# Decay buffers taken strictly in turn, decays first in ScalarE's order, and four steps of the plan moved by one scan

## The chip, the core and the metric

The kernel runs on one core of one Trainium2 chip. The metric is the device time of one execution in microseconds. Before the change, the median of three runs is 29332.89 us (29323.41 to 29336.83).

The engines are named as in the profile: PE (TensorE, with PEld for its weight loads), DVE (VectorE), ACT (ScalarE), POOL (GpSimd) and SP (SyncE, which here issues all DMAs). Each engine works through its own queue in order, so an instruction that waits holds up all that stand behind it on that engine.

## What is computed

The input is eight images of 64 channels by 128 by 128. Two layers follow each other. Cut to what matters here:

```
# layer 0: a learned high-pass filter, nine weights a pixel
h    = leaky(conv3x3(x, w1));  w_lp = softmax(conv1x1(h, w2) over the 9 taps)
x    = x + sum over taps of shifted(x) * (delta - w_lp)
# layer 1: norms, then two bidirectional state space blocks over the 16384 pixels of an image
for each block, for each direction:
    xc = silu(causal_conv1d(x));  dt = softplus(...);  B, C = projections of xc
    state[d, n] = exp(dt[d] * A[d, n]) * state[d, n] + dt[d] * B[n] * xc[d]     # along the pixels
    y[d] = sum over n of state[d, n] * C[n] + D[d] * xc[d];  y *= silu(z)
# then "mix": two 3x3 convolutions, a product and a norm; then an FFN:
g = depthwise3x3(conv1x1(x, 340 channels));  out = x + conv1x1(gelu(g1) * g2)
```

With 128 channels d and 16 states n there are 2048 recurrences a direction, each 16384 pixels long.

## The kernel before, in words

**Chunks and scans.** The recurrences run on DVE. A chunk is 1024 pixels of one direction of one block of one image; there are 512 chunks, each with 16 scans of 128 recurrences by 1024 pixels, so 8192 scans in all. Scan `u` of a chunk needs:

- `decay` (L1118): one ACT instruction that writes exp(dt * A) into a PSUM tile `w` of two banks;
- `drive` (L1110): POOL's product `bu` of dt * xc and B, one instruction for two scans, four buffers;
- `scan` (L1136 forwards, L1138 backwards): one DVE instruction. Its result goes into the tile `hs` if POOL is to multiply by C, else back into `w` in place;
- `product` by C: on POOL (L1157, about a third of the scans: u even, not 4 or 12, and 8 only beside other work), else on DVE (L1160), from `w` into `hs`;
- `keep` (L1150): a small ACT copy of the last column into `state`. For a POOL product it stands right after the scan and POOL waits for it; for a DVE product it stands after the product;
- `collect` (L1176): PE sums over n into a PSUM tile `y`, which `y_out` reads in halves (L1193 on ACT in a first direction, L1191 on DVE in a second one).

**One time axis.** All work is placed by hand: `at(time, phase, step)`, where a unit of time is one scan and scan `u` of a chunk that begins at `b` stands at `b + u`. Steps are issued in order of time, within a time by phase (FEED, SCAN, MID, PROD, DECAY, REST), and within a phase in the order of the calls. That gives each engine's queue. `decay(u)` stands at `b + u - 2`, two scans ahead, in phase DECAY, behind what an earlier chunk put into the same time and phase.

**The two buffers of `w`.** The tiles come from a pool of PSUM with two buffers under one tag (`ps_w`, tag "w"), and the framework gives each new tile the buffer that its own scheduling model expects to be free first. In the program as built, 7773 decays get the other buffer than the decay before them, and 419 get the same one: 377 of these at u = 3 or u = 11, all of them after a scan whose product is on POOL. A decay in the same buffer has to wait until the scan just before its own has read it.

**Beside the scans** three streams of other work run, each at its own time of the image (an image is 1024 scans): the *front* of the next image (layer 0 and the first norms, one piece each 24 scans, times 569 to 985 of an image), the *mix* of the image itself (a piece each 13 scans, from time 992 for 208 scans, so into the next image's first 176) and the *FFN* of the image before (a piece each 24 scans, times 180 to 569). Their convolutions are PE work. Of the front, the softmax over taps matters here: `less_max` on DVE and `exps` (L539) on ACT at time b + 23, `sums` (L543, L544: a reduction and a reciprocal on DVE) at b + 24, `softmax` (L547 on POOL) at b + 24, then three `piece`s (L551 on ACT) with `less_piece` (L555 on POOL) between them, and a PE transposition. Of the FFN: four parts of `conv` (L819, L825 on PE) at a + 14 to a + 17 fill two PSUM banks, `times` (L881, two DVE products with the gelu) at a + 19 reads them, `project` (PE) at a + 19, `add` (L903 on ACT) and `store` at a + 21.

**DMAs.** SP issues everything, in order. The tiles of C (`load_states("cp", ...)`, L1088, four DMAs of 256 KB for half of the states) have one buffer a half; the half that a chunk needs from its scan 4 on is loaded at time b, after the last product of the chunk before has read the old one.

At the start nine pieces of the front and at the end the last FFN stand alone, without scans beside them; they use the `ps_w` buffers too.

Of the kernel before, what the change touches and what calls it, by code (L numbers as in the profile page):

```python
# [8 lines left out]
F32 = mybir.dt.float32  # L9
# [4 lines left out]
PSUM = bass.MemoryType.PSUM  # L14

P = 128
# [14 lines left out]
T = 1024  # L31
# [2 lines left out]
G = 4  # L34
U = G * G
PW = W + 2
FEED, SCAN, MID, PROD, DECAY, REST = range(6)

IMAGE = 4 * NT * U
FRONT_STEP, MIX_STEP, FFN_STEP = 24, 13, 24  # L40
# [2 lines left out]
SILU, SOFTPLUS, GELU = 11, 18, 11  # L43
# [12 lines left out]
def kernel(ctx: ExitStack, tc: tile.TileContext, a: dict, out: bass.AP):  # L56
# [134 lines left out]
    with tc.tile_pool(name="wspill", bufs=1) as fp, tc.tile_pool(name="wprep", bufs=2) as pp, \  # L191
            tc.tile_pool(name="wps", bufs=4, space=PSUM) as pps:
        with tc.manual_schedule():
# [126 lines left out]
            for l in range(DEPTH):  # L320
# [17 lines left out]
                for d in range(2):  # L338
# [3 lines left out]
                    for j in range(KC):  # L342
                        t = turned(taps[:, j, :], ident, P, DI)
                        at = j if d == 0 else KC - 1 - j
# [51 lines left out]
    def at(time, phase, fn, *args):  # L396
        steps.setdefault((time, phase), []).append((fn, args))
# [1 line left out]
    inp = ctx.enter_context(tc.tile_pool(name="in", bufs=2))  # L399
    wk = ctx.enter_context(tc.tile_pool(name="wk", bufs=2))  # L400
    sd = ctx.enter_context(tc.tile_pool(name="between", bufs=3, space=bass.MemoryType.DRAM))
    pw = ctx.enter_context(tc.tile_pool(name="ps_w", bufs=2, space=PSUM))
    py = ctx.enter_context(tc.tile_pool(name="ps_y", bufs=1, space=PSUM))
    pm = ctx.enter_context(tc.tile_pool(name="ps_mm", bufs=1, space=PSUM))
    pb = ctx.enter_context(tc.tile_pool(name="ps_bg", bufs=1, space=PSUM))
    pa = ctx.enter_context(tc.tile_pool(name="ps_acc", bufs=1, space=PSUM))

    def mm_tile(name):
        return pm.tile([P, N], F32, tag="mm", name=name)
# [87 lines left out]
    class Front:  # L497
# [68 lines left out]
        def weight(self, k):  # L566
            if not self.alone:
                self.wb = bg_tile("wb")
            else:
                if k % 2 == 0:  # L570
                    self.wbs = pw.tile([P, T], F32, tag="w", name="wb")
                self.wb = self.wbs[:, N * (k % 2) : N * (k % 2) + N]
            self.wbk[k] = self.wb
            nc.tensor.matmul(self.wb, sel_k[:, k].rearrange("k h c -> k (h c)"), self.wt, start=True, stop=True)
# [73 lines left out]
        def plan(self, a):  # L648
            n1, n2, n3 = self.n1, self.n2, self.n3
            b = a - FRONT_STEP  # L650
            self.alone = a + FRONT_STEP < -2
            at(b - 5, REST, self.load_xa)
            for i in range(3):
                at(b + 1 + i, REST, self.hidden, i)
            at(b + 6, DECAY, self.hidden_out)
            at(b + 21, REST, self.logits)
            at(b + 23, DECAY, self.less_max)
            at(b + 23, DECAY, self.exps)
            at(b + 24, DECAY, self.sums)
            at(b + 24, REST, self.softmax)  # L660
            for i in range(3):
                at(b + 26 + 2 * i, DECAY, self.piece, i)
                if i < 2:
                    at(b + 27 + 2 * i, REST, self.less_piece, i)
            at(b + 31, REST, self.turn)
            at(b + 32, DECAY, self.turned)
            at(a + 6, REST, self.load_xb)
            for k in range(9):

                t = a + k + (k >= 3)  # L670
                at(t + 11, REST, self.weight, k)
                at(t + 12, MID, self.weighted, k)
                at(t + 13, REST, self.gather, k)
            at(a + 23, DECAY, self.filtered)
            at(a + 23, REST, self.store_x1)
            at(a + 23, REST, self.centered, acc_tile, "x1")
            at(a + 24, DECAY, self.centered_out)
            at(a + 25, REST, lambda: n1.means(bg_tile, self.sq))
            at(a + 26, DECAY, n1.means_out)
            at(a + 26, REST, n1.root)  # L680
            at(a + 28, REST, n1.spread, bg_tile)
            at(a + 29, MID, self.scaled, n1)
            at(a + 29, DECAY, self.first_norm)
            at(a + 30, REST, self.pointwise)
            at(a + 31, DECAY, self.pointwise_out)
            at(a + 31, REST, self.store_rows, dw_img[self.p], "dwt")
            at(a + 31, REST, self.centered, acc_tile, "xn")
            at(a + 32, DECAY, self.centered_out)
            at(a + 33, REST, lambda: n2.means(acc_tile, self.sq))
            at(a + 34, DECAY, n2.means_out)  # L690
            at(a + 34, REST, n2.root)
            at(a + 36, REST, n2.spread, acc_tile)
            at(a + 37, MID, self.scaled, n2)
            at(a + 37, DECAY, self.second_norm)
            at(a + 37, REST, self.store_h)
            at(a + 38, REST, lambda: n3.means(bg_tile, self.sq))
            at(a + 39, DECAY, n3.means_out)
            at(a + 39, REST, n3.root)
            at(a + 47, REST, n3.spread, bg_tile)
            at(a + 49, MID, self.third_norm)  # L700
            at(a + 49, REST, self.store_hn)
# [81 lines left out]
    class Ffn:  # L783
# [15 lines left out]
        def conv(self, g, part):  # L799

            wpair, wlast, _, _, _, _ = ffn_weights(Bg.weights)
            if part == 0 and self.alone:
                w = pw.tile([P, T], F32, tag="w", name="fp")
                self.p = [w[:, 0:N], w[:, N:T]]
            elif part == 0:
                self.p = [acc_tile("fp"), bg_tile("fp")]
            if g == 2:
                self.rest = self.p
            outs = []
            for h in range(2):  # L810
                if g < 2:
                    outs += [(self.p[h], h, slice(0, P))]
                else:
                    outs += [(self.p[0][C * h : C * h + C, :], h, slice(C, P))]
            for h in range(2 * (g == 2)):
                outs += [(self.p[1][C * h : C * h + C, :], h, slice(0, C))]
            for i in ((0,), (1,), (2,), ())[part]:
                for o, h, m in outs:
                    nc.tensor.matmul(  # L819
                        o, wpair[:, i, g, m], self.win[h][:, i : i + ROWS, 0:W], start=(i == 0), stop=False  # L820
                    )
            for i in ((), (), (0,), (1, 2))[part]:
                for o, h, m in outs:
                    rows, lo = slice(C * h, C * h + C), 2 - h
                    nc.tensor.matmul(  # L825
                        o, wlast[rows, i, g, m], self.win[h][rows, i : i + ROWS, lo : W + lo],
                        start=False, stop=(i == 2),
                    )
# [83 lines left out]
        def plan(self, a):  # L912
            early = 12 if self.alone else 0
            at(a - 4 - early, REST, self.load, 0)
            at(a - 3 - early, REST, self.load, 1)

            if self.alone:
                at(a - 6, REST, self.before_taps)
                at(a - 5, DECAY, self.before_taps_out)
                at(a - 5, REST, self.taps, 0)  # L920
                at(a - 2, REST, self.taps, 1)
                groups = ((0, 0, self.first_out, 2), (3, 1, self.times, 6))
                gelus, out = 3, 9
            else:
                groups = ((0, 0, self.first_out, 5), (6, 2, None, 0), (14, 1, self.times, 19))
                gelus, out = GELU, 19
            for t, g, end, to in groups:
                for i in range(4):
                    at(a + t + (0 if self.alone else i), REST, self.conv, g, i)
                for h in range(2 if end else 0):  # L930
                    at(a + to, MID if end == self.times else DECAY, end, h)
            at(a + gelus, REST, self.gelus)
            at(a + gelus + 2, MID, self.rest_times)
            at(a + out - 5, REST, self.load_x2)
            at(a + out, REST, self.project)
            at(a + out + 2, DECAY, self.add)
            at(a + out + 2, REST, self.store)
# [15 lines left out]
    class Chunk:  # L953
# [159 lines left out]
        def decay(self, u):  # L1113
            k, i = divmod(u, 2)
            j, gp = self.pairs[k]
            g = 2 * gp + i
            w = pw.tile([P, T], F32, tag="w", name="w")
            nc.scalar.activation(  # L1118
                w, self.dtp[gp][:, i, :], AF.Exp, scale=a_neg[:, self.l, self.d, g, j : j + 1]
            )  # L1120
            self.ws[u] = w
# [115 lines left out]
        def plan(self):  # L1237
            b = self.t0 - 2 * U
# [20 lines left out]
            b = self.t0  # L1259
# [11 lines left out]
            at(b - 4, REST, self.load_states, "cp", j0)  # L1271
            at(b - 3, REST, self.load_channels, "dup", 1)
            at(b - 2, REST, self.load_channels, "dtp", 1)
            at(b + 0, REST, self.load_states, "cp", 1 - j0)
            for k in range(U // 2):
                at(b + 2 * k - 5, REST, self.drive, k)
                at(b + 2 * k + 3 + (k % 4 == 0), REST, self.collect, k)
            for u in range(U):
                at(b + u - 2, DECAY, self.decay, u)
                at(b + u, SCAN, self.scan, u)  # L1280
                at(b + u + self.on_pool(u), FEED if self.on_pool(u) else PROD, self.product, u)
            for h in range(2):
# [76 lines left out]
```

## Time and profile before

| what | value |
|---|---|
| median of three runs | 29332.89 us |
| the profiled execution's own time | 29319.34 us |
| span of its profile | 29317.6 us |
| PE busy | 23234.6 us (79%) |
| DVE busy | 27195.5 us (93%) |
| ACT busy | 18546.6 us (63%) |
| POOL busy | 27646.8 us (94%) |
| decays, L1118 on ACT | 8192 of 1118 ns (median) |
| scans, L1136 and L1138 on DVE | 8192 of about 2345 ns |
| products, L1160 on DVE and L1157 on POOL | 5360 of 1221 ns and 2832 of 2358 ns |
| drives, L1110 on POOL | 4096 of 4538 ns |
| DMA engines, mean busy share of the hardware queue | 71.0% |
| first scan and last scan start | 507 us and 28869 us |

The profile is one execution. Its page gives the busy time of each engine, which counts neither semaphores nor the issuing of DMAs, then groups of instructions with the idle time of the engine just before them and what ended that. The view of waits sums this by pairs: "engine line waited for: us in total, times, longest us". A window is a stretch of the span in us. A time line has the start, the duration, the engine and line, and in square brackets the idle time before and its releaser.

### The profile page before, as it was taken

How to read it: one execution, taken by the hardware profiler on the slowest of the kernel's cores; microseconds unless marked ns; L12 is line 12 of the kernel's file. 1: busy time of each engine (PE TensorE's matmuls, PEld its weight loads, DVE VectorE, ACT ScalarE, POOL GpSimd, SP SyncE). 2: the span in 40 equal slices, each digit the busy share in tenths (PEclk: the TensorE clock that was granted, in tenths of full speed). 3: DMA queues.
4: the chain of work that ended last, by engine and by line, in shares of the span. 5: the costliest groups of instructions: out<-in, count | busy, mean ns of one | idle time of the engine just before them, and what ended most of it. 6: DMA issues, size and time to landing. Idle time of an engine off the chain costs nothing. (4 is left out here: it accounts for less than half of the span.)

```text
span 29317.6 us, 309769 instructions
## 1 busy us (share of the span) xinstructions
PE 23234.6 (79%) x97708; PEld 7300.4 (25%) x97708; DVE 27195.5 (93%) x17567; ACT 18546.6 (63%) x28361; POOL 27646.8 (94%) x8732
## 2 busy tenths in 40 slices
PE   6666888878788787887878778787787877878678
PEld 3211222222222222222322223222222222222123
DVE  4999999999999999999999999999999999999997
ACT  3666666666666666666666666666666666666663
POOL 3999999999999999999999999999999999999994
PEclk7777888988899888998889889898888988889789
DMA  4676777767777678776787767777677776777674
GB/s 121 224 241 217 228 250 244 239 218 230 253 240 238 216 234 258 239 237 214 234 258 240 233 217 239 252 241 230 218 240 252 240 228 220 246 249 238 218 250 142
DMA packets 2592261, 6762.65 MB, mean 231 GB/s; under 512 B 431270, under 2 KB 736822, under 8 KB 2589462
## 3 DMA queue, kind: packets, MB, share of 16 engines
q1 hardware_dynamic: 2590614, 6742.83, 71.0%
q8 instruction: 773, 12.66, 0.2%
q14 instruction: 874, 7.16, 0.1%
HBM read 5509.49 MB, written 1265.19 MB: 231 GB/s over the span
## 5 line engine op out<-in xcount | busy, mean ns | idle before, releaser
L1110 POOL TENSOR_TENSOR bu<-dup,bp 128x2048 f32<-128x2048 f32 x4096 | 18558.9, 4538 | 15.9 <-DMA dup<-du_dram 7.2
L1118 ACT ACTIVATE w<-dtp,a_neg 128x1024 f32<-128x1024 f32 x8192 | 9159.0, 1118 | 750.6 <-DVE hs L1136 360.6
L1157 POOL TENSOR_TENSOR hs<-hs,cp 128x1024 f32<-128x1024 f32 x2832 | 6679.1, 2358 | 618.0 <-ACT state L1150 557.5
L1160 DVE TENSOR_TENSOR hs<-w,cp 128x1024 f32<-128x1024 f32 x5360 | 6546.4, 1221 | 254.9 <-DMA cp<-bc_dram 73.2
L1136 DVE TENSOR_TENSOR_SCAN w<-w,state,bu 128x1024 f32<-128x1024 f32 x2677 | 6280.0, 2346 | 313.5 <-ACT w L1118 311.9
L1138 DVE TENSOR_TENSOR_SCAN w<-w,state,bu 128x1024 f32<-128x1024 f32 x2683 | 6289.6, 2344 | 293.8 <-ACT w L1118 292.7
L1176 PE MATMUL y<-hs,sel_y 128*32 128x512 f32 x32768 | 5055.5, 691 | 66.8 <-POOL hs L1157 66.4
L1150 ACT COPY state<-w 128x1 f32<-128x1 f32 x5360 | 837.1, 156 | 5943.6 <-DVE hs L1160 5873.0
L1138 DVE TENSOR_TENSOR_SCAN hs<-w,state,bu 128x1024 f32<-128x1024 f32 x1413 | 3308.1, 2341 | 145.8 <-issue 57.7
L1136 DVE TENSOR_TENSOR_SCAN hs<-w,state,bu 128x1024 f32<-128x1024 f32 x1419 | 3321.0, 2340 | 64.4 <-ACT state L1150 45.5
L987 PE MATMUL xp<-hn,wx 128*128 128x512 f32 x4096 | 2396.1, 715 | 690.3 <-ACT xc L993 469.4
L1169 PE MATMUL y<-xc,dskip 128*64 128x512 f32 x4096 | 1483.7, 812 | 1404.9 <-ACT yv L1193 1329.5
L819 PE MATMUL fp<-fw,bgw 128*128 128x512 f32 (+1 forms) x5760 | 2236.9, 629 | 108.4 <-ACT ga L866 84.9
L1028 PE MATMUL dp<-xc,wdt 128*128 128x512 f32 x2048 | 1242.3, 691 | 631.2 <-ACT dt L1035 385.2
L478 POOL TENSOR_TENSOR r<-r,neg_half 128x8 f32<-128x8 f32 x768 | 1263.0, 1645 | 373.8 <-ACT r L475 340.1
L1176 PEld LDWEIGHTS y<-hs,sel_y 128*32 128x32 f32 x32768 | 723.3, 116 | 3567.9 <-issue 2503.5
L1118 ACT ACT_TABLE_LOAD x1134 | 1454.9, 1283 | 20.2
L1150 ACT COPY state<-hs 128x1 f32<-128x1 f32 x2832 | 540.9, 191 | 1460.8 <-DVE hs L1138 792.1
L825 PE MATMUL fp<-fw,bgw 64*128 64x512 f32 (+1 forms) x5760 | 1419.1, 611 | 0.0
L589 PE MATMUL acc<-t,ident 128*128 128x512 f32 x2160 | 1283.8, 678 | 159.3 <-DVE hc L609 157.3
L987 PEld LDWEIGHTS xp<-hn,wx 128*128 128x128 f32 x4096 | 856.5, 223 | 2058.1 <-issue 966.9
L993 ACT ACTIVATE xc<-xp,cbias 128x512 f32<-128x512 f32 x1024 | 695.5, 679 | 942.0 <-PE xp L987 939.8
(214 smaller groups left out, 26173.3 us busy)
## 6 DMA issues: line engine op xcount, KB each, us to landing
bp<-bc_dram SPq DMA_DIRECT2D x4096, 256.0 KB, 4.1
dup<-du_dram SPq DMA_DIRECT2D x4096, 256.0 KB, 5.1
dtp<-dt_dram SPq DMA_DIRECT2D x4096, 256.0 KB, 5.0
cp<-bc_dram SPq DMA_DIRECT2D x4096, 256.0 KB, 4.8
hn<-hn_dram SPq DMA_DIRECT2D x1024, 256.5 KB, 4.4
dt_dram<-dt SPq DMA_DIRECT2D x512, 512.0 KB, 3.0
du_dram<-du SPq DMA_DIRECT2D x512, 512.0 KB, 2.6
yf_dram<-yv SPq DMA_DIRECT2D x512, 256.0 KB, 4.4
```

The lines of the kernel that those rows point to most:

```text
L819: nc.tensor.matmul(o, wpair[:, i, g, m], self.win[h][:, i : i + ROWS, 0:W], start=(i == 0), stop=False)
L825: nc.tensor.matmul(o, wlast[rows, i, g, m], self.win[h][rows, i : i + ROWS, lo : W + lo], start=False, stop=(i == 2),)
L987: nc.tensor.matmul(self.xp[h], wx[:, self.l, self.d, i, :], self.hn2[:, s.start + 2 * i : s.stop + 2 * i], start=(i == 0), stop=(i == 1),)
L1110: nc.gpsimd.tensor_tensor(bu, self.dup[self.pairs[k][1]], self.over_pair("bp", k), ALU.mult)
L1118: nc.scalar.activation(w, self.dtp[gp][:, i, :], AF.Exp, scale=a_neg[:, self.l, self.d, g, j : j + 1])
L1136: nc.vector.tensor_tensor_scan(to, w, bu, s0, ALU.mult, ALU.add)
L1138: nc.vector.tensor_tensor_scan(to[:, ::-1], w[:, ::-1], bu[:, ::-1], s0, ALU.mult, ALU.add)
L1150: nc.scalar.copy(self.column(u), h[:, T - 1 : T] if self.d == 0 else h[:, 0:1])
L1157: nc.gpsimd.tensor_tensor(hs, hs, c, ALU.mult)
L1160: nc.vector.tensor_tensor(hs, w, c, ALU.mult)
L1169: nc.tensor.matmul(self.y[C * h : C * h + C, :], dskip[:, self.l, self.d, C * gp : C * gp + C], self.xc[:, s], start=True, stop=False,)
L1176: nc.tensor.matmul(self.y[lo : lo + 32, :], sel_y, hs[:, i, s], start=False, stop=(k % 4 == 3))
```

## The change

- `ps_w` gets one buffer a tag and two tags, `w0` and `w1`; a helper `w_tile` takes them strictly in turn, for decays and for the two other users of the pool.
- A phase EXP is put between PROD and DECAY, and `decay` goes into it: among the steps of one time it now stands ahead of all ACT work of phase DECAY. In the built program this moves decays ahead of 256 `y_out` copies, of the `residual` and `square` of 256 chunks, of their `means_out`, and of 128 `weighted`.
- `sums` and `softmax` of the front stand at b + 25 instead of b + 24, and `sums` in phase MID (after the scan, ahead of the product).
- `times` of the FFN stands at a + 20 instead of a + 19; `project`, `load_x2`, `add` and `store` follow by one too.
- The second half of C is loaded at b - 1 instead of b.

No instruction is added or removed, and POOL's order is the same in both programs.

```diff
-FEED, SCAN, MID, PROD, DECAY, REST = range(6)
+FEED, SCAN, MID, PROD, EXP, DECAY, REST = range(7)
...
-    pw = ctx.enter_context(tc.tile_pool(name="ps_w", bufs=2, space=PSUM))
+    pw = ctx.enter_context(tc.tile_pool(name="ps_w", bufs=1, space=PSUM))
...
+    turn = [0]
+
+    def w_tile(name):
+        turn[0] ^= 1
+        return pw.tile([P, T], F32, tag=f"w{turn[0]}", name=name)
...
-                    self.wbs = pw.tile([P, T], F32, tag="w", name="wb")
+                    self.wbs = w_tile("wb")
...
-            at(b + 24, DECAY, self.sums)
-            at(b + 24, REST, self.softmax)
+            at(b + 25, MID, self.sums)
+            at(b + 25, REST, self.softmax)
...
-                w = pw.tile([P, T], F32, tag="w", name="fp")
+                w = w_tile("fp")
...
-                groups = ((0, 0, self.first_out, 5), (6, 2, None, 0), (14, 1, self.times, 19))
-                gelus, out = GELU, 19
+                groups = ((0, 0, self.first_out, 5), (6, 2, None, 0), (14, 1, self.times, 20))
+                gelus, out = GELU, 20
...
-            w = pw.tile([P, T], F32, tag="w", name="w")
+            w = w_tile("w")
...
-            at(b + 0, REST, self.load_states, "cp", 1 - j0)
+            at(b - 1, REST, self.load_states, "cp", 1 - j0)
...
-                at(b + u - 2, DECAY, self.decay, u)
+                at(b + u - 2, EXP, self.decay, u)
```

## The prediction

> **What bounds the kernel now.** I read the page's busy times first.
>
> ```profile
> PE 23234.6 (79%) x97708; PEld 7300.4 (25%) x97708; DVE 27195.5 (93%) x17567; ACT 18546.6 (63%) x28361; POOL 27646.8 (94%) x8732
> ```
>
> POOL and DVE are almost equally full. The change takes no work from either, so it can only fill gaps. Next, busy time by stage of one image: FFN, front, mix.
>
> ```profile
> 8244.00:9571.00 1327.00, 1121.57 (x4513) 334.22 (x4514) 1252.68 (x747) 879.46 (x1287) 1266.09 (x368) 0.93 0.73 237
> 9571.00:11066.00 1495.00, 1179.98 (x5161) 401.44 (x5162) 1400.93 (x971) 964.72 (x1538) 1460.23 (x497) 0.86 0.68 223
> 11066.00:11806.00 740.00, 581.72 (x2600) 164.09 (x2598) 703.25 (x412) 474.04 (x715) 736.85 (x232) 0.88 0.82 263
> ```
>
> After the length come PE, PEld, DVE, ACT, POOL, then clock, DMA share and GB/s. POOL idles 60.9 us in the FFN, 34.8 in the front, 3.2 in the mix. From the first scan to the end of the last (507 to 28870, 28363 us) it is busy 27572.7, so 790 us are the ceiling for filling gaps there. The head (507 us) and the tail (448 us, PE busy 420) have no scans; the edits barely touch them. POOL's waits over the whole span:
>
> ```profile
> POOL hs L1157 <- ACT state L1150: 557.5, 550, 4.5
> POOL r L478 <- ACT r L475: 340.1, 117, 18.0
> POOL lg L547 <- DVE sm L544: 251.9, 9, 155.0
> ```
>
> The third and 218 us of the second belong to head and tail (122.0 of it remains from 500 to 28850). The first is POOL waiting for a `keep`, which waits for a scan: DVE was late, or the `keep` stood behind a decay on ACT. DVE hardly ever waits for POOL (bu, 40.3 us in all). So outside the mix DVE sets the pace, and its waits count. First in the FFN stage, then in the front:
>
> ```profile
> DVE w L1138 <- ACT w L1118: 20.2, 17, 1.2
> DVE ga L881 <- PE fp L825: 13.3, 11, 2.2
> DVE hs L1160 <- DMA cp<-bc_dram: 8.1, 3, 5.9
> DVE w L1136 <- ACT w L1118: 2.4, 2, 1.2
> ```
>
> ```profile
> DVE w L1138 <- ACT w L1118: 19.3, 12, 3.0
> DVE w L1136 <- ACT w L1118: 17.5, 15, 2.2
> DVE sm L543 <- ACT lg L539: 16.0, 6, 3.2
> DVE sm L543 <- ACT state L1150: 3.5, 2, 1.8
> ```
>
> **Edit 1, the buffers.** The time line around scan 11 of a chunk in the FFN shows what sharing costs; ACT, then DVE:
>
> ```profile
> 8263.36 0.69 ACT L993 ACTIVATE xc<-xp,cbias 128x512 f32<-128x512 f32 x1 [2.63 <-PE xp L987]
> 8263.94 0.15 ACT L1150 COPY state<-w 128x1 f32<-128x1 f32 x1
> 8265.28 1.12 ACT L1118 ACTIVATE w<-dtp,a_neg 128x1024 f32<-128x1024 f32 x1 [1.19 <-DVE hs L1136]
> ```
>
> ```profile
> 8262.91 2.34 DVE L1136 TENSOR_TENSOR_SCAN hs<-w,state,bu 128x1024 f32<-128x1024 f32 x1
> 8266.44 2.36 DVE L1136 TENSOR_TENSOR_SCAN w<-w,state,bu 128x1024 f32<-128x1024 f32 x1 [1.19 <-ACT w L1118]
> ```
>
> ACT is free at 8264.09, but `decay(11)` has scan 10's buffer and waits for that scan's end at 8265.25; DVE then stands idle for 1.19 us while it runs. Taken in turn, it would start at 8264.1 in scan 9's buffer and end with scan 10, at 8265.2; scan 10's `keep`, which stands behind it and two copies at 8267.29, would come about 1.2 us earlier too. Next late is then DVE's own work. It pays only where ACT stood idle. ACT's waits of a decay for a scan, two rows of the FFN, then two of the front:
>
> ```profile
> ACT w L1118 <- DVE hs L1138: 27.4, 17, 2.1
> ACT w L1118 <- DVE hs L1136: 3.3, 2, 2.1
> ```
>
> ```profile
> ACT w L1118 <- DVE hs L1136: 4.5, 3, 2.1
> ACT w L1118 <- DVE hs L1138: 3.6, 2, 2.1
> ```
>
> FFN: 19 decays idled 1.6 us on average, DVE lost 22.6 after them; I take 19. Front: only 5 did, worth 6 of the 36.8 us; the others come from an ACT that is late itself (it waits 72.4 us there for `xp` from PE), and stay. Mix: 20 decays (39.6 us of ACT idling), but POOL has 3.2 us to give; I take 1. In the first image's stretch without FFN (1242 to 2443) DVE waits 23.8 us for decays, 20 times, POOL idles 34.2 and waits 26.2 for keeps: I take 20.
>
> **Edit 2, decays first.** What they pass: a `y_out` copy (0.584 us, 256 times), `residual` and `square` (0.579 and 0.601, 256), `means_out` (0.262, 256), `weighted` (0.724, 128). The decay gains at most 0.6 to 1.2 us, felt only where DVE waits for it; the others lose 1.12 us, and `y_out` 2.40 us where a load of the exp table (1.28) goes ahead with the decay. Behind `y_out` waits PE's single `y` tile: PE and PEld already wait for it (1329.5 us of PE's idling), then all of PE's queue. Only chunks of a first direction have this copy: some 9 in an FFN stage, 9 x 2.40 = 22 us against 205 us that PE idles, and 12 in a front, 29 us against 315. The gain is at most the 37 us that DVE waits for decays in a front, the loss at most those 22 and 29 us; PE's idle time is the nearest row and covers the loss, the late ACT work in the front is mostly not what is passed, so I take zero.
>
> In the trace a load of 1.28 us (8271.93) is followed by its activation at 8273.22, at once. The Trainium skill, "ScalarE: Activation LUTs", section "What ACT_TABLE_LOAD costs", adds a drain of about 1380 ns to each switch; an estimate by it would make `y_out` 3.8 us late instead of 2.40. The trace shows no such gap.
>
> **Edit 3, softmax sums.** In the front DVE stands 19.5 us (8 waits) at L543 for `exps`, which ACT issues late. A scan (2.35) now comes first. A wait of 3.1 us is not saved whole: after it the next scan's decay, 1.12 us behind `exps` on ACT, is late next. At one of them the product ends at 9903.80 and `exps` at 9906.87, `decay(11)` at 9908.08. Scan 10 would now run to 9906.1, the sums wait 0.8 us and end at 9907.3, and scan 11 starts at 9908.1 instead of 9910.09: 2.0 us of 3.11. The same reckoning at the wait of 1.78 us at 10432.4 gives 1.6. So 4 x 2.0 + 4 x 1.6 = 14 us a stage. POOL's `softmax` comes no earlier in its queue. There recip ended at 9907.37 and POOL took it up at 9909.4; where `exps` was in time the sums shift by a scan and the slack nearly goes: up to 0.5 us for 8 of 16 a stage, 4 us at most, taken as zero.
>
> **Edit 4, gelu product.** Its waits are at most 2.2 us in this stage, shorter than the scan that moves ahead: 13.3 us go, I take 12. PE's `project` waits for it as before; `add` frees its bank a scan (about 3.4 us) later, with two scans left before the next piece; if that cover were gone, PE would wait up to 3.4 us a piece, 16 x 3.4 = 54 us a stage at worst. On SP the load of `x2` and the store move with it, past a few loads; nobody waits for the store.
>
> **Edit 5, C.** 8.1 us in the FFN (5.9 of it once). A scan earlier saves at most 3.4 of the large one, and SP holds the load until the old C is read; 4 us, between 0 and 8.1. In the built order it passes two loads of the front's window (`xb`, needed six scans later) and some of the mix; SP waits for DVE's last product at this line already (50.8 us, 23 times in the FFN stage), so these loads come at most that 2.2 us later.
>
> **The sum.** FFN: 19 + 12 + 4 = 35 us of DVE; POOL waits 56.7 us there for keeps, so nearly all passes on: 33. Front: 6 + 14 = 20, POOL waits 18.3 for keeps and 14.6 for `r`: 15. Seven of each: 231 + 105. Mix 7 x 1 = 7. First image's rest 20, its front beside image 0's start (735 us, POOL idle 22.4) 10, last image's end (27389 to 28870, idle 18.9) 5. Together 378 us: 29319.3 - 378 = 28941 for an execution like the profiled one; the median lies 13.5 above that, so about 28955.
>
> **The rivals.**
>
> (a) POOL sets the pace. The Trainium skill, "Perfetto Trace Analysis", section "Identifying the Most-Contended Engine", says to improve the engine of highest occupancy first; by that POOL, whose work stays, and the gain would be near nothing. POOL's 790 us of gaps speak against it, the mix for it. If DVE's gains only lengthen its lead, what is left is POOL starting earlier after a same-buffer decay, which now stands ahead of the `keep`: about half of the 419 at 1.12 us at most, less where POOL had no gap; 60 to 250 us. Chance 0.18, about 29180.
>
> (b) The gaps close nearly all: the 557 us for keeps and part of `r` go, since each stall on DVE is felt again later. 560 to 700 us, about 28710. Chance 0.05.
>
> (c) Slower: `y_out` behind decay and table load holds PE, and PE's late convolutions hold DVE, which waits 250.0 us for `wb` already. 256 x 2.40 = 614 us if all of it arrives, against 378: 29570. It decides from 1.5 us for each copy. Against it: PE idles 15 to 21% of the stages. Chance 0.09.
>
> (d) No difference: the framework's choice of buffers was only a name, or the gains and costs cancel. The 1.19 us on both engines speak against it. 29333 us, chance 0.05.
>
> **Numbers.** The forecast (250 to 560 us gained) has the remaining 0.63. Faster 0.86, within 0.2% (59 us, about what a measurement here can tell from nothing) 0.05, slower 0.09. The range 28720 to 29230 (613 to 103 us gained) takes in all of the forecast, most of (a) and half of (b), 0.80.
>
> **What would show it.** Right: ACT waits of L1118 for L1136 and L1138 (621 us) gone; DVE's waits for `w` (604.6 us) down to some 260, most in the front; L543's 172.8 us mostly gone, L881's below 40; POOL's wait for keeps down to 150 to 250; the FFN stage near 1294 us, the front near 1480, the mix the same 740. Wrong: POOL's keep waits as before (a), or `wb` and `y` waits on PE and DVE grown by hundreds (c).

## The result, and the profile after

The changed kernel takes 29402.75 us (median of 12 runs, 29387.12 to 29409.67), the kernel before, in the same rounds, 29334.86 us (12 runs, 29323.41 to 29344.63). The ratio is 1.0023, 95% interval 1.0014 to 1.0031: slower by 68 us, where 378 us less were forecast. The prediction was wrong, and in sign.

The busy times of the page after:

```profile
PE 23282.5 (79%) x97708; PEld 7345.4 (25%) x97708; DVE 27214.2 (93%) x17567; ACT 18632.1 (63%) x28361; POOL 27640.7 (94%) x8732
```

The work is the same, as the diff says; only the gaps moved. Windows of the FFN and the front stage beside image 2 (columns as before):

```profile
8240.00:9572.00 1332.00, 1135.12 (x4524) 345.10 (x4524) 1253.86 (x747) 882.07 (x1285) 1266.59 (x368) 0.91 0.74 236
9572.00:11082.00 1510.00, 1182.69 (x5168) 403.31 (x5160) 1403.36 (x971) 968.41 (x1539) 1459.58 (x497) 0.85 0.68 221
```

Forecast were some 1294 and 1480 us; they are 1332 and 1510. Yet most of the waits that the change set out to shorten did shrink. No decay waits for a scan any more: the 621 us of ACT at that pair are gone altogether. DVE's waits after, over the whole span:

```profile
DVE t L584 <- PE wb L580: 398.5, 215, 12.7
DVE hc L615 <- PE rb L490: 240.0, 122, 12.0
DVE w L1142 <- ACT w L1124: 185.4, 178, 3.3
DVE w L1144 <- ACT w L1124: 182.2, 149, 3.3
DVE hs L1144 <- PE y L1182: 112.9, 66, 3.6
...
DVE ga L887 <- PE fp L831: 27.7, 14, 6.9
```

(Six lines of code were added: L1124 after is L1118 before, and so on.) The waits for `w` fell from 604.6 to 367.6 us, the gelu product's from 124.9 to 27.7, the softmax sums' from 172.8 to 7.9 (5.0 for `exps` and 2.9 for a `keep` on ACT). Only DVE's wait for the loads of C, which edit 5 aimed at, did not fall: 80.4 us after, 73.2 before. In place of the others DVE waits for PE: for `wb`, the broadcast weights, 398.5 instead of 250.0; for `rb`, the spread of a norm's factors, 240.0 instead of 147.3; for `y` 112.9 instead of 9.6 at L1144. And PE waits for ACT:

```profile
PE y L1175 <- ACT yv L1199: 1777.7, 403, 14.0
...
PE dp L1034 <- ACT r L481: 355.1, 146, 6.8
PE xp L993 <- ACT sq L1224: 330.0, 93, 6.4
```

These three were 1329.5, 241.9 and 133.1 us. The ACT instructions named, `y_out`, `means_out` and `square`, are three of those that the decays now pass. POOL's waits answer to that:

```profile
POOL hs L1163 <- ACT state L1156: 554.1, 357, 4.1
POOL r L484 <- ACT r L481: 420.0, 182, 17.5
```

The first, POOL waiting for a `keep`, was to fall from 557.5 to 150 to 250 and did not move; the second grew from 340.1.

### The profile page after: what moved, and what is told of

It is laid out like the page before. It is cut to its first block, busy times and chain, and to the rows that moved or that the text cites. A ratio compares the mean times of both kernels' runs of the same rounds, so it can differ in the third digit from the quotient of the medians.

```text
span 29385.3 us, 310056 instructions
## 1 busy us (share of the span) xinstructions
PE 23282.5 (79%) x97708; PEld 7345.4 (25%) x97708; DVE 27214.2 (93%) x17567; ACT 18632.1 (63%) x28361; POOL 27640.7 (94%) x8732
## 5 line engine op out<-in xcount | busy, mean ns | idle before, releaser
L1124 ACT ACTIVATE w<-dtp,a_neg 128x1024 f32<-128x1024 f32 x8192 | 9159.1, 1118 | 160.9 <-DMA dtp<-dt_dram 5.4
L1163 POOL TENSOR_TENSOR hs<-hs,cp 128x1024 f32<-128x1024 f32 x2832 | 6715.3, 2371 | 627.7 <-ACT state L1156 554.1
L1166 DVE TENSOR_TENSOR hs<-w,cp 128x1024 f32<-128x1024 f32 x5360 | 6545.6, 1221 | 259.3 <-DMA cp<-bc_dram 80.4
L1144 DVE TENSOR_TENSOR_SCAN w<-w,state,bu 128x1024 f32<-128x1024 f32 x2683 | 6287.3, 2343 | 183.6 <-ACT w L1124 182.2
L1144 DVE TENSOR_TENSOR_SCAN hs<-w,state,bu 128x1024 f32<-128x1024 f32 x1413 | 3310.9, 2343 | 310.1 <-PE y L1182 112.9
L1175 PE MATMUL y<-xc,dskip 128*64 128x512 f32 x4096 | 1482.6, 811 | 1843.5 <-ACT yv L1199 1777.7
L825 PE MATMUL fp<-fw,bgw 128*128 128x512 f32 (+1 forms) x5760 | 2334.8, 649 | 25.9 <-ACT ga L872 12.4
L1034 PE MATMUL dp<-xc,wdt 128*128 128x512 f32 x2048 | 1265.2, 703 | 679.6 <-ACT r L481 355.1
```

Of the source, the lines that this page charges most:

```text
L825: nc.tensor.matmul(o, wpair[:, i, g, m], self.win[h][:, i : i + ROWS, 0:W], start=(i == 0), stop=False)
L1124: nc.scalar.activation(w, self.dtp[gp][:, i, :], AF.Exp, scale=a_neg[:, self.l, self.d, g, j : j + 1])
L1144: nc.vector.tensor_tensor_scan(to[:, ::-1], w[:, ::-1], bu[:, ::-1], s0, ALU.mult, ALU.add)
L1163: nc.gpsimd.tensor_tensor(hs, hs, c, ALU.mult)
L1166: nc.vector.tensor_tensor(hs, w, c, ALU.mult)
L1175: nc.tensor.matmul(self.y[C * h : C * h + C, :], dskip[:, self.l, self.d, C * gp : C * gp + C], self.xc[:, s], start=True, stop=False,)
```

## The experiments

All were timed in five rounds against the kernel before on the same chip (its median 29364 to 29376 us there); each ratio has its 95% interval, about 0.13% to each side, so a difference of two ratios is good to about 0.18%. The rounds ran on two chips, and the kernel before took 29 to 41 us more in them than in the result's rounds (29334.86), so kernels from different rounds are compared by their ratios. The theory: the order on ACT (edit 2) costs more than the other four edits bring, because ACT copies that free a PSUM tile now stand behind a decay. The first rival: the strict turn, not the order, costs the time. The second: the four edits bring little and the order little.

**The buffers alone.** The kernel before with edit 1.

```diff
-    pw = ctx.enter_context(tc.tile_pool(name="ps_w", bufs=2, space=PSUM))
+    pw = ctx.enter_context(tc.tile_pool(name="ps_w", bufs=1, space=PSUM))
...
+    def w_tile(name):
+        turn[0] ^= 1
+        return pw.tile([P, T], F32, tag=f"w{turn[0]}", name=name)
...
-            w = pw.tile([P, T], F32, tag="w", name="w")
+            w = w_tile("w")
...
```

> The kernel before with edit 1 alone: the two PSUM buffers of the decays taken strictly in turn. Theory O (the order: decays first is what costs, because ACT's copies behind them hold PE): the turn is a gain by itself, 29335 less 100 to 250, about 29160, and POOL's wait for keeps falls below 450 us. Theory L (late: the gelu product, the projection and the softmax a scan later are what costs): the same 29160. Theory B (the turn itself brings nothing, because what a decay gains is lost on the next thing that ACT or PE is late with): 29320 to 29400, with DVE's waits for w about halved as in the kernel after, and the keep wait near 557 us.

Measured 29164.48 us, ratio 0.9931 [0.9919, 0.9944]. The turn is a gain of 206 us (202 were put for it in the FFN, the front, the mix and the first image's rest), so the first rival falls.

**The order alone.** The kernel before with edit 2.

```diff
-FEED, SCAN, MID, PROD, DECAY, REST = range(6)
+FEED, SCAN, MID, PROD, EXP, DECAY, REST = range(7)
...
-                at(b + u - 2, DECAY, self.decay, u)
+                at(b + u - 2, EXP, self.decay, u)
```

> The kernel before with edit 2 alone: the decays ahead of the other ACT work of the same time; the buffers stay with the framework (419 decays still share). Theory O: slower by the price of the order, 29335 plus 100 to 250, about 29480, with PE's waits for y_out (1330 us before, 1778 after) near 1780. Theory L and theory B: 29320 to 29360.

Measured 29794.74 us, ratio 1.0144 [1.013, 1.0158]. One line of the plan costs 424 us, more than all other edits were forecast to bring, and well over the 100 to 250 expected here. PE's wait for `yv` is 1874.7 us here, DVE's for `wb` 380.2, POOL's for keeps 813.1.

**All but the order.** The changed kernel with the decay back in phase DECAY.

```diff
-FEED, SCAN, MID, PROD, EXP, DECAY, REST = range(7)
+FEED, SCAN, MID, PROD, DECAY, REST = range(6)
...
-                at(b + u - 2, EXP, self.decay, u)
+                at(b + u - 2, DECAY, self.decay, u)
```

> The kernel after without edit 2: turn, sums, gelu product and C moved, the decays in phase DECAY as before. Theory O: all gains and no price, 29050 to 29200; PE's wait for y_out back to about 1330 us. Theory L: as slow as after, about 29400. Theory B: between, 29300 to 29350.

Measured 28933.18 us (28929.03 to 28934.51), ratio 0.9851 [0.9836, 0.9866], faster than any of the expectations: with the last experiment below, which is equal to it, the best version of all, 1.49% below the kernel before (437 us by the medians on that chip, where 378 were forecast for the whole change). So the price of the order within the changed kernel is 1.0023 - 0.9851 = 1.72%, some 505 us of the 29371 that the kernel before takes there. A wait of PE, one of POOL and one of DVE in its trace:

```profile
PE y L1175 <- ACT yv L1199: 1263.5, 360, 11.5
```

```profile
POOL hs L1163 <- ACT state L1156: 237.8, 246, 4.1
```

```profile
DVE t L584 <- PE wb L580: 240.8, 142, 12.7
```

`dp` behind `r` is 210.1 and `xp` behind `sq` 215.6 us here. POOL's keeps are inside the 150 to 250 us that the prediction named.

**Which of the passed copies costs.** Four kernels put part of ACT's work ahead of the decays or back behind them. First `y_out` alone ahead again:

```diff
-                    at(b + 8 * h + 11, DECAY, self.y_out, h)
+                    at(b + 8 * h + 11, EXP, self.y_out, h)
```

> The kernel after, with y_out of a first direction put into the phase of the decays, where it stands ahead of them as in the kernel before; residual, square, means_out and weighted stay behind the decays. Theory O with y_out as the culprit: nearly as e3, 29100 to 29250. Theory O with the others as culprits: 29350 to 29400. Theories L and B: 29380 to 29400.

Measured 29219.42 us, ratio 0.9947 [0.9935, 0.996]. That takes back 0.76 of the 1.72%, not all: other copies matter as much. The complement, only `y_out` behind the decays:

```diff
-            at(b + 6, DECAY, self.residual)
-            at(b + 6, DECAY, self.square)
+            at(b + 6, EXP, self.residual)
+            at(b + 6, EXP, self.square)
...
-            at(b + 13, DECAY, n.means_out)
+            at(b + 13, EXP, n.means_out)
...
-                at(b + 20, DECAY, self.weighted)
+                at(b + 20, EXP, self.weighted)
```

> The kernel after, with residual, square, means_out and weighted put into the phase of the decays, where they stand ahead of them again; only y_out stays behind its decay (and behind the load of the exp table). So far, as ratios to before: after 1.0023, without edit 2 0.9851, with y_out ahead 0.9947. Theory A (each copy behind a decay has its own price): 0.985 plus 0.0076 = 0.9927. Theory J (they act together: one late release makes the next one late): 0.996 to 1.000, since y_out alone then already costs most of it.

Measured 29138.27 us, ratio 0.9921 [0.9909, 0.9934], so 0.70% over the kernel without the order, about 205 us or 0.8 us a copy. Then `y_out`, `residual` and `square` ahead, `means_out` and `weighted` behind:

```diff
-                    at(b + 8 * h + 11, DECAY, self.y_out, h)
+                    at(b + 8 * h + 11, EXP, self.y_out, h)
...
-            at(b + 6, DECAY, self.residual)
-            at(b + 6, DECAY, self.square)
+            at(b + 6, EXP, self.residual)
+            at(b + 6, EXP, self.square)
```

> The kernel after, with y_out, residual and square ahead of the decays; only means_out and weighted stay behind. Of the 1.7% that the order costs, y_out ahead gave 0.76% back, 0.96% is left. Theory S (residual and square: they free the PSUM bank that PE's next convolution xp waits for, and ACT then waits for xp): about 0.986. Theory M (means_out: it frees the same bank for dp, and POOL's r waits for it): 0.990 to 0.994.

Measured 29077.11 us, ratio 0.9902 [0.9889, 0.9916]: `residual` and `square` are worth 0.9947 - 0.9902 = 0.45%. And with `means_out` ahead as well (the edit on top of the last), only `weighted` behind:

```diff
-            at(b + 13, DECAY, n.means_out)
+            at(b + 13, EXP, n.means_out)
```

> As e6 (0.9902), with means_out ahead of the decay too, so that of edit 2 only weighted (0.724 us, 128 times, nothing on PE reads it) stays behind. Theory M (means_out holds the PSUM bank that PE's dp waits for): back to the level without edit 2, 0.9845 to 0.986. If weighted has a price of its own: 0.988 to 0.990.

Measured 28946.99 us, ratio 0.9853 [0.9839, 0.9866]: `means_out`, 256 activations of a quarter of a microsecond, is worth 0.49%, and `weighted` 0.02%, not told from nothing. With `y_out` at 0.76 the four prices add up to the whole 1.72% by the way they are taken, step after step; with its price from the other end, 0.70, to 1.66%, so here it matters little in which order the copies go back. In each step PE's wait at the tile in question falls with the time: PE's waits in us, over each whole trace:

| kernel | `y` for `yv` | `xp` for `sq` | `dp` for `r` |
|---|---|---|---|
| all behind the decays (after) | 1777.7 | 330.0 | 355.1 |
| `y_out` ahead | 1287.7 | 332.5 | 357.3 |
| `residual`, `square` ahead too | 1282.0 | 225.5 | 384.1 |
| `means_out` ahead too | 1257.6 | 206.1 | 203.7 |
| the decays behind (without edit 2) | 1263.5 | 215.6 | 210.1 |

What DVE and POOL then wait for, in us, and whether PE was slower (its busy time and mean granted clock):

| kernel | POOL for keeps | POOL `r` for ACT's `r` | DVE `t` for `wb` | DVE scan (L1144) for `y` | PE busy | clock |
|---|---|---|---|---|---|---|
| all behind the decays (after) | 554.1 | 420.0 | 398.5 | 112.9 | 23282.5 | 0.865 |
| `y_out` ahead | 441.1 | 353.1 | 244.8 | 115.2 | 23258.8 | 0.869 |
| `residual`, `square` ahead too | 292.7 | 341.5 | 244.9 | 49.1 | 23141.5 | 0.874 |
| `means_out` ahead too | 237.8 | 292.5 | 239.2 | 11.1 | 23158.8 | 0.875 |
| the decays behind (without edit 2) | 237.8 | 294.1 | 240.8 | 7.5 | 23141.6 | 0.875 |

So `y_out` is felt at `wb` and at the keeps, `residual` and `square` at POOL's keeps and at the scans that wait for `y`, `means_out` at the keeps, at POOL's `r` and at those scans.

**The same place in two traces** shows the path for `y_out`: scans 660 and 661 of image 2, counted from 0 (scans 4 and 5 of a chunk), in the front, where a load of the exp table goes with the decay. First with only `y_out` behind, then without edit 2; start, duration, engine, all in order of time.

```profile
9836.00 2.35 DVE L1144 TENSOR_TENSOR_SCAN w<-w,state,bu 128x1024 f32<-128x1024 f32 x1
...
9836.29 1.28 ACT L1124 ACT_TABLE_LOAD   x1
9837.59 1.12 ACT L1124 ACTIVATE w<-dtp,a_neg 128x1024 f32<-128x1024 f32 x1
...
9838.64 0.58 ACT L1199 COPY yv<-y 128x512 f32<-128x512 f32 x1
...
9839.27 1.98 PE L1175 MATMUL y<-xc,dskip 128*64 128x512 f32 x4 [3.68 <-ACT yv L1199]
...
9839.97 2.35 DVE L1144 TENSOR_TENSOR_SCAN w<-w,state,bu 128x1024 f32<-128x1024 f32 x1
...
9844.59 0.38 PE L580 MATMUL wb<-wt,sel_k 65*128 65x512 bf16 x1
...
9845.01 0.69 DVE L584 TENSOR_TENSOR t<-xb,wb 128x512 f32<-128x512 f32 x1 [2.68 <-PE wb L580]
```

```profile
9754.84 2.35 DVE L1144 TENSOR_TENSOR_SCAN w<-w,state,bu 128x1024 f32<-128x1024 f32 x1
...
9755.05 0.59 ACT L1199 COPY yv<-y 128x512 f32<-128x512 f32 x1
...
9755.68 1.97 PE L1175 MATMUL y<-xc,dskip 128*64 128x512 f32 x4 [1.25 <-ACT yv L1199]
...
9758.82 2.35 DVE L1144 TENSOR_TENSOR_SCAN w<-w,state,bu 128x1024 f32<-128x1024 f32 x1
...
9760.74 0.38 PE L580 MATMUL wb<-wt,sel_k 65*128 65x512 bf16 x1
...
9761.15 0.69 DVE L584 TENSOR_TENSOR t<-xb,wb 128x512 f32<-128x512 f32 x1
```

Counted from the start of scan 660, `y` begins at 3.27 instead of 0.84 us, `wb` at 8.59 instead of 5.90, and DVE stands 2.68 us. In the good order `wb` is done at 9761.12 and DVE, just through with scan 661, takes it up at 9761.15: PE idled 1.25 us in front of `y`, but the chain behind it had nothing to spare. Over the whole trace DVE's wait for `wb` is 393.7 us with `y_out` behind, against 240.8. At one step of a chunk, that of the time line (ahead of scan 6, when the `y_out` that ends the chunk before has run beside scan 4), it is 153 us in 62 waits against 4 us in 8: that step holds nearly all the growth.

**Too late instead of too early.** The kernel without edit 2, with the decays behind all other work of their phase (the edit against the changed kernel, where the decays stand in EXP):

```diff
-FEED, SCAN, MID, PROD, EXP, DECAY, REST = range(7)
+FEED, SCAN, MID, PROD, DECAY, EXP, REST = range(7)
```

> Without edit 2 (0.9851), and the decays moved the other way: behind all ACT work of phase DECAY of the same time, that of later chunks (conv_out, step_out, gate_out, bc_out) and of front, mix and FFN too. Theory O carried on (whatever frees a PSUM bank for PE should go first, a decay two scans ahead has time): faster still, 0.975 to 0.984, with PE's waits for ACT below those of e3. Rival (the decays are what DVE waits for; only a short piece of ACT work may pass them): slower, 0.990 to 1.000, with DVE's waits for w (312 us in e3) grown by 150 or more.

Measured 29443.98 us, ratio 1.0026 [1.0017, 1.0035]: 1.75% over the old order, as dear as too early, and by another path. The theory as carried on, which had it faster still, is wrong: not everything on ACT does well to go ahead of a decay. DVE's waits for decays nearly double (312.1 us without edit 2):

```profile
DVE w L1142 <- ACT w L1124: 328.3, 297, 3.2
DVE w L1144 <- ACT w L1124: 265.9, 205, 3.8
```

Its waits for keeps grow from 72.2 to 485.7 us (248.9 and 236.8), while that for `wb` falls to 157.5. The old order, in which a decay stands between what an earlier chunk and a later call put into the phase, has worse neighbours on both sides.

**The other edits, each with the turn.** Alone, they would also have changed how the framework picks the buffers (454 to 477 same-buffer decays instead of 419 with the product or the sums moved), so each stands on edit 1.

```diff
-            at(b + 0, REST, self.load_states, "cp", 1 - j0)
+            at(b - 1, REST, self.load_states, "cp", 1 - j0)
```

> Edits 1 and 5 alone: the turn (0.9931) and the second half of C loaded a scan earlier. By the prediction edit 5 is worth 28 us, 0.1%: 0.9921. Theory of no gain (SP holds the load until the old C is read anyway): 0.9931. If the loads that it passes come too late: above 0.994.

Measured 29133.13 us, ratio 0.9921 [0.9908, 0.9935], 0.10% below the turn alone: not told from nothing.

```diff
-            at(b + 24, DECAY, self.sums)
-            at(b + 24, REST, self.softmax)
+            at(b + 25, MID, self.sums)
+            at(b + 25, REST, self.softmax)
```

> Edits 1 and 3 alone: the turn (0.9931) and the softmax sums a scan later. By the prediction edit 3 is worth 14 us a front stage on DVE, some 12 after passing on, seven and a half stages: 90 us, 0.3%: 0.990. Theory of a moved wait (ACT's late exps hold the next decay just as long): 0.9925 to 0.9935.

Measured 29054.31 us, ratio 0.9891 [0.9877, 0.9904]: the sums bring 0.40%.

```diff
-                groups = ((0, 0, self.first_out, 5), (6, 2, None, 0), (14, 1, self.times, 19))
-                gelus, out = GELU, 19
+                groups = ((0, 0, self.first_out, 5), (6, 2, None, 0), (14, 1, self.times, 20))
+                gelus, out = GELU, 20
```

> Edits 1 and 4 alone: the turn (0.9931) and the gelu product a scan later. By the prediction edit 4 is worth 12 us an FFN stage, seven stages: 84 us, 0.3%: 0.990. Theory of a moved wait (PE or ACT later by a scan behind it): 0.9925 to 0.994.

Measured 29069.0 us, ratio 0.9896 [0.9883, 0.991]: the product brings 0.35%. The four gains add: 0.69 + 0.10 + 0.40 + 0.35 = 1.54%, against 1.49% for all of them together. The second rival falls with that, on both its counts. Three gains are each told from nothing, that of C is not.

**Does `y_out` gain by being earlier still?** The kernel without edit 2, with the ACT copy and its store a scan sooner.

```diff
-                    at(b + 8 * h + 11, DECAY, self.y_out, h)
-                    at(b + 8 * h + 12, REST, self.store_y, h)
+                    at(b + 8 * h + 10, DECAY, self.y_out, h)
+                    at(b + 8 * h + 11, REST, self.store_y, h)
```

> Without edit 2 (0.9851), and y_out of a first direction placed one scan earlier, ahead of the softplus and its table loads on ACT: its release of the y tile comes some 3.5 us earlier. Theory O carried on (the release to PE is what counts): PE's wait for y_out falls from 1264 us below 800, time 0.980 to 0.984. Rival (ACT now waits for PE's last collect, and the decays behind it are late): 0.987 to 0.995, with ACT waiting for y by 100 us or more.

Measured 28931.82 us, ratio 0.9849 [0.9836, 0.9862]: no change, which neither expectation had. PE's wait there falls by 908 us:

```profile
PE y L1175 <- ACT yv L1199: 355.0, 165, 8.6
```

and comes back elsewhere: `dp` behind `dt` 492.9 instead of 312.1, `rb` behind POOL's `r` 466.7 instead of 219.8, `y` behind POOL's products 416.7 instead of 169.0. So hundreds of microseconds of PE waiting for `y` cost nothing here, where DVE's wait for `wb` is 216.7 us against 240.8; the 536 us more of it with only `y_out` behind the decays (1799.6) cost some 205, and there that wait grew by 152.9. That the due time of `wb` makes the difference fits both runs and the time lines; it was not set apart by a run of its own.

## Why the prediction was wrong

**Edits 1, 3, 4, 5: right, and nearly to size** (437 us on one chip, 378 forecast; the mechanism was right for 1, 3 and 4). Stage times, summed over the seven images, worked out from the start of the scans at the stages' ends in each trace (us):

| kernel | FFN | front | mix | first image's rest |
|---|---|---|---|---|
| before | 9281.9 | 10475.1 | 5189.6 | 1200.3 |
| without edit 2 | 9053.9 | 10358.7 | 5170.5 | 1178.5 |
| difference (forecast) | -228 (-231) | -116 (-105) | -19 (-7) | -22 (-20) |
| after | 9321.0 | 10554.1 | 5153.6 | 1176.8 |

The trace of the kernel before is from other rounds than that without edit 2, and in the latter rounds the kernel before took longer, so the differences in this table come out some 45 us small in all (390 us between the two spans, 437 by the medians on one chip). By edits: the turn took 112 us from the FFN and 28 from the front (forecast 133 and 42), and 22 from the mix and 18 from the rest; the sums 99 from the front (98); the product 99 from the FFN (84). Only C is smaller on its trace, 4 us in the FFN where 28 were put, and DVE's wait for C did not go: it is 73.2 us before, 138.9 with the turn alone and 125.3 with C moved as well. Probably DVE, held up less elsewhere, comes to C sooner; no run shows that. With edit 2 left out the FFN stage is 9053.9 / 7 = 1293 us and the front 1480, as named beforehand. The loads that edit 5 passes were said to come "at most" 2.2 us later; that is the mean of SP's 23 waits, the longest was 5.0. Nothing else rested on it. One named size was off: the waits for `w` stay at 312.1 us without edit 2, not 260.

**Edit 2: the step that failed** is "PE's idle time is the nearest row and covers the loss, ... so I take zero". Measured, the order costs 1.72%, some 505 us. Two things were wrong in it.

First, the row. That PE idles 205 us in an FFN stage says that work could be put there by someone, not that a delay is taken up by it. PE idles because its queue is in order and many of its matmuls wait for another engine's result; the instructions behind them are due at a fixed time on DVE. What had to be asked was when `wb` is needed and when it comes: 9761.12 against 9761.15 in the time line above. `y_out` was priced at up to 22 + 29 us a pair of stages, and what arrived lies within that: FFN 62 and front 127 us over the run, 189 / 7 = 27 us a pair (only `y_out` behind, against without edit 2).

Second, what was left out of the sum. `residual`, `square` and `means_out` were listed with 1.12 us of delay and followed no further. Each ends a tenure of the one-buffer tile `mm`, and `means_out` also begins the chain `r`, POOL's power, `rb` and the block's own `hn` on DVE. From the stage times, `residual` and `square` cost 124 us in the FFN and nothing told in the front (-5), `means_out` 92 and 68. Together they are more than `y_out` (0.94% against 0.70 to 0.76%).

**What edit 2 was to gain** was bounded by the 37 us that DVE waits for decays in a front. After, these waits are 18.2 and 18.6 us in the front window: not a microsecond of it came. Those decays were late for another reason than what they passed, as the prediction said.

**The rivals.** (c), `y_out` behind decay and load holding PE and then `wb`, is what happened in kind; its sign to look for, `wb` and `y` waits grown by hundreds (by 148.5 and 448.2 us), is there. Its price was off in both directions: 614 us for `y_out` at 2.40 each, where 0.8 each arrived, and nothing for the other three copies, which brought the rest. Its condition, 1.5 us a copy, was not met, and the sign turned all the same. (a), POOL sets the pace, is refuted, since without edit 2 the gain is 437 us where it gave at most 250: POOL's own work is 27631.7 to 27653.3 us in kernels of 28947 and of 29795 us, and in the best one its keep waits fell to 237.8. (b), the gaps close nearly all, did not come either: 237.8 us for keeps and 294.1 for `r` are left there. (d) had two halves. That the choice of buffers was only a name is refuted by the turn's 0.69%; that gains and costs cancel is nearly what happened, 1.49% against 1.72%, and its 29333 us is the rival's figure nearest to the result, though it named neither the cost nor its place.

The Trainium skill, "Perfetto Trace Analysis", section "Identifying the Most-Contended Engine", would have the engine of highest occupancy improved first. In these runs no work was taken from POOL, the fullest, and the time moved over a range of 3%; the engine whose order decided was ACT, at 62 to 64%.

**What stays open.** The path from `y_out` over `wb` to DVE is shown in the time line and in the count at scan 6. It is a path of the front; the 62 us that `y_out` costs in the FFN stages, where DVE has no `wb` to wait for, go another way: DVE's wait for the gelu's `gt`, 30.6 instead of 4.0 us, is a part of it, and the rest was not followed. For `residual`, `square` and `means_out` the price, PE's wait at the tile and the waits of DVE and POOL that change with it are shown, but not the path of one delay from end to end. `means_out`'s own chain is not where it costs: DVE's `hn` waits 17.0 us for `rb` with it behind and 13.1 with it ahead, while `hc` of the other streams goes from 232.4 to 187.6.

Whether some of the loss is a slower clock: the granted clock is 0.865 after, 0.861 with the order alone and 0.875 before and without edit 2. For `y_out` and `means_out` a slower PE is not the cause. With only `y_out` behind, PE is busy 23100.5 us, less than the 23141.6 without edit 2, and with `means_out` and `weighted` behind 23141.5, and yet these kernels take 0.70 and 0.51% longer. For `residual` and `square` it is not separated: putting them ahead takes 128 us from PE's busy time in the seven FFN stages (7938.8 to 7811.1, clock 0.914 and 0.929), as much as the 124 us by which these stages get shorter. The clock may be the path there, or follow from the changed order; no run tells.

## What to carry to other kernels

Idle time of an in-order engine is no cover for a delay: to price one, follow the queue behind the delayed instruction to the first result that another engine needs, and compare when it comes with when it is due. Where an engine does both, try the short copies that give back a single PSUM tile ahead of long work with two steps of lead, but not all other work ahead of it (that cost as much here), and price every instruction that a reordering passes, the 0.26 us ones too. Where a change has several parts, take the order apart from the rest: here four parts gave 1.5% and one line took back 1.7%.

## What the runs showed of the hardware that was not expected

Gains and losses of a few tenths of a per cent added up in a kernel whose engines wait for each other everywhere: 1.54 against 1.49% for the gains, 1.66 against 1.72% for the losses. Such sums are good to some 0.3%, so the closeness is in part luck. And a wait of 1263.5 us, the longest of PE's, could be cut to 355.0 with no measurable effect on the time, while the 0.26 us activation `means_out`, 256 times, moved it by 0.49%, about 144 us, or twice its own busy time (256 x 0.26 = 67 us).
